# Two chunks of a two-layer kernel: written-out engine lists, a projection loaded in quarters, and two small matmul groups placed elsewhere

## The chip, the cores and the metric

The kernel runs on one core of one Trainium2 chip. The metric is the device time of one execution in microseconds (us). The program's engines run side by side, each through its own list of instructions in order: TensorE (PE, with its weight loads as PEld), VectorE (DVE), ScalarE (ACT), GpSimd (POOL) and SyncE (SP, which here only issues transfers).

## The reference

A residual stream x of 16 x 256 tokens with 256 features goes through two layers, all in float32. The first layer, where the whole change lies, is:

```
xn = layernorm(x)
s  = recurrence(xn)                      # B projection, complex decay over 256 steps,
                                         # C projection, plus D * xn
g  = silu(gelu(xn @ proj1.T + b1) @ proj2.T + b2)
x  = x + s * g
```

The hidden width is 1024 and the recurrence has 32 complex states per sequence; its B is scaled by a gain, its decay and angle come from two small parameter vectors. The second layer has the same frame, with multi-head latent attention (16 heads, causal) as s and a routed low-rank projection as g.

## The kernel before

The 4096 tokens are cut into 8 chunks of 512, that is two sequences, and x stays in SBUF for the whole run. Layer 0 goes chunk by chunk:

- `norm0` makes xn (statistics and the final scaling on VectorE, the power -0.5 on GpSimd as `rs`), `turn0` transposes it on TensorE to `xnT`.
- `hidden` makes the 8 blocks of the first projection (`ph` in PSUM) from `p1T` and `xnT`; ScalarE takes each through Gelu to `hT`. The PSUM pool `ps_mm` has four buffers, so TensorE can run four blocks ahead of ScalarE.
- `recur` multiplies by the turned B (`bT`) into `pb`, and VectorE and GpSimd run the scan to `hs`.
- `mix` makes half of the second projection (`pf`, two PSUM buffers), VectorE adds the bias to get `zf`, ScalarE applies Silu.
- `outs` multiplies `hs` by `csc` into two PSUM buffers `py` (pool `ps_y`, two buffers in all), GpSimd makes `dx = xn * D`, and VectorE adds `py` to it. `finish0` multiplies by `zf` and adds to x, on GpSimd.
- `fold_heads` folds weights of layer 1 (matmuls `psq` and `pso`) in the first four chunks.

The first chunk is special. `start` loads x in four pieces, computes statistics and projections by halves of the chunk, and interleaves VectorE's long list of tiny operations that make the recurrence's parameters (`later.write`): from `par` the exponent, the angle and the gain; then `gsq` (a square root as a power, on GpSimd), `gs`, the scaled B `bsc`, then `rot`, `ct`, `stb`, `sns`, `decay`, `csc`. `turn_b` transposes `bsc` into `psb` and ScalarE copies it to `bT`.

TensorE's order is always the order in which the program is written (`pe` is an `InOrder`, whose call helper is line 53, so most instructions are shown there). In the first chunk VectorE (`v0`), GpSimd (`g0`), ScalarE (`a0`) and SyncE (`s0`) have such lists too, but not for every instruction: those written on `nc.scalar`, `nc.gpsimd` or `nc.vector` directly are placed by a scheduler. In the program before, the order around the change is: on TensorE `pf` of chunk 0 first half, `psb`, `pf` second half, `ph` of chunk 1, `pb`, and so on; on ScalarE both Silus of chunk 0 ahead of the eight Gelus of chunk 1; on GpSimd the four copies `wrope<-wraw` of `load_layer1` (line 147) ahead of `gsq`; in chunk 1 `py` of chunk 0, the transposes of chunk 2, `py` of chunk 1, then the second half of `pf`.

Of the kernel before, what the change touches and what calls it, by code (L numbers as in the profile page):

```python
# [11 lines left out]
F32 = mybir.dt.float32  # L12
I32 = mybir.dt.int32
AF = mybir.ActivationFunctionType
ALU = mybir.AluOpType
# [3 lines left out]
P = 128  # L19
B, S, D = 16, 256, 256  # L20
# [5 lines left out]
FF = 1024  # L26
# [15 lines left out]
def tile_two_layers(ctx: ExitStack, tc: tile.TileContext, d: dict, out: bass.AP):  # L42
    nc = tc.nc
# [96 lines left out]
    rb_bc = w1.tile([P, NE], F32, tag="rb_bc", name="rb_bc")  # L140
    kvw_bc = w1.tile([P, KVL], F32, tag="kvw_bc", name="kvw_bc")

    def load_layer1(wraw):
        nc.sync.dma_start(wraw, d["wq_rope"].rearrange("(c p) n f -> p c n f", p=P))
        for c in range(2):
            for r in range(2):
                nc.gpsimd.tensor_copy(
                    wrope[:, c, :, r, :, :],
                    wraw[:, c, :, HR * r : HR * r + HR].rearrange("p (g h) f -> p g h f", h=4),
                )  # L150
        nc.sync.dma_start(wkva, d["wkv_a"].rearrange("(c p) f -> p c f", p=P))
        nc.sync.dma_start(wmid, d["w_mid"].rearrange("(c p) f -> p c f", p=P))
        nc.sync.dma_start(wbase, d["base_wT"].rearrange("(c p) f -> p c f", p=P))
        nc.sync.dma_start(wlb, d["lora_B"])
        nc.sync.dma_start(bb_bc, d["base_b"].partition_broadcast(P))
        nc.sync.dma_start(rb_bc, d["router_b"].partition_broadcast(P))
        nc.sync.dma_start(kvw_bc, d["kv_norm_w"].partition_broadcast(P))

        nc.sync.dma_start(rot_q[0:64, 0, :], d["rope_q"][0:64, 1, :])
        nc.sync.dma_start(rot_q[64:128, 0, :], d["rope_q"][64:128, 0, :])  # L160
        for h in range(4):
            nc.sync.dma_start(rot_q[32 * h : 32 * h + 32, 1, :], d["rope_q"][32:64, 2, :])
        nc.sync.dma_start(rope_k, d["rope_k"])
        nc.sync.dma_start(desc, d["desc"])
# [33 lines left out]
    def bc(ap, n):  # L198

        return ap.unsqueeze(1).to_broadcast([ap.shape[0], n, ap.shape[1]])  # L200
# [6 lines left out]
    with ExitStack() as l0:  # L207
# [3 lines left out]
        a2 = l0.enter_context(tc.tile_pool(name="a0", bufs=2))  # L211
# [5 lines left out]
        wraw = stage.tile([P, 2, NH, ROPE], F32, tag="wraw", name="wraw", bufs=1)  # L217
        p1T = w0.tile([P, 2, FF], F32, tag="p1T", name="p1T")
        p2T = w0.tile([P, NFC, D], F32, tag="p2T", name="p2T")
        b1 = w0.tile([P, NFC], F32, tag="b1", name="b1")  # L220
        b2_bc = w0.tile([P, D], F32, tag="b2_bc", name="b2_bc")
        d_bc = w0.tile([P, D], F32, tag="d_bc", name="d_bc")
# [5 lines left out]
        p1d = d["proj1T"].rearrange("(c p) f -> p c f", p=P)  # L228
        p2d = d["proj2T"].rearrange("(c p) f -> p c f", p=P)
        s0 = InOrder(nc.sync)  # L230
        a0 = InOrder(nc.scalar)
        a0.dma_start(par, d["par"])
        a0.dma_start(b1, d["proj1_b"])
        for j in range(TPC):
            s0.dma_start(X[0][:, j, :], x_dram[j * P : (j + 1) * P, :])
        for z, e in ((0, a0), (1, s0)):
            fz = slice(z * FF // 2, (z + 1) * FF // 2)
            e.dma_start(p1T[:, :, fz], p1d[:, :, fz])
        a0.dma_start(sgn, d["signs"])
        s0.dma_start(bst, d["B_stack"][0 : 2 * NST, :])  # L240
        load_x(1, s0)
# [25 lines left out]
        g0 = InOrder(nc.gpsimd)  # L267
# [72 lines left out]
        f = tiny("f")  # L340
# [12 lines left out]
        for k in range(1, 8):  # L353
            c, s = rot[:, k - 1, 0:1], rot[:, k - 1, 1:2]
# [10 lines left out]
        for k in range(8):  # L365
            n = 1 << k
            c, s = rot[:, k, 0:1], rot[:, k, 1:2]
# [63 lines left out]
        def hidden(ch, xnT):  # L431
            hT = []
            for fc in range(NFC):
                ph = ps_mm.tile([P, CH], F32, tag="mm", name=f"ph_{ch}_{fc}")
                for c in range(2):
                    pe.matmul(
                        ph, p1T[:, c, fc * P : (fc + 1) * P], xnT[:, c, :],
                        start=(c == 0), stop=(c == 1),
                    )
                ht = hpool.tile([P, CH], F32, tag="hT", name=f"hT_{ch}_{fc}")  # L440
                nc.scalar.activation(ht, ph, AF.Gelu, bias=b1[:, fc : fc + 1])  # L441
                hT.append(ht)
            return hT

# [9 lines left out]
        def recur(ch, xnT):  # L454

            pb = ps_mm.tile([P, S], F32, tag="mm", name=f"pb_{ch}")
            for c in range(2):
                for b in range(2):
                    pe.matmul(
                        pb[64 * b : 64 * b + 64, :], bT[:, c, :],  # L460
                        xnT[:, c, b * S : (b + 1) * S], start=(c == 0), stop=(c == 1),
                    )

            v = a2.tile([P, S], F32, tag="v", name=f"v_{ch}")
            w = a2.tile([P, S], F32, tag="w", name=f"w_{ch}")
            v0.tensor_tensor(v, pb, ct, ALU.mult)
            swapped(w, pb)
            nc.gpsimd.tensor_tensor(v, v, w, ALU.add)
            g = a2.tile([P, S], F32, tag="g", name=f"g_{ch}")
            nc.vector.tensor_tensor_scan(g, decay, v, 0.0, ALU.mult, ALU.add)  # L470
            swapped(w, g)
            h = a2.tile([P, S], F32, tag="hs", name=f"hs_{ch}")
            nc.vector.tensor_tensor(h, g, ct, ALU.mult)
            nc.gpsimd.tensor_tensor(h, h, w, ALU.subtract)
            return h

        def mix(ch, jp, hT):
            pf = ps_f.tile([P, 2, D], F32, tag="pf", name=f"pf_{ch}_{jp}")
            for j2 in range(2):
                cols = slice((2 * jp + j2) * P, (2 * jp + j2 + 1) * P)  # L480
                for fc in range(NFC):
                    pe.matmul(
                        pf[:, j2, :], hT[fc][:, cols], p2T[:, fc, :],
                        start=(fc == 0), stop=(fc == NFC - 1),
                    )
            zf = a2.tile([P, 2, D], F32, tag="zf", name=f"zf_{ch}_{jp}", bufs=3)
            nc.vector.tensor_tensor(zf, pf, bc(b2_bc, 2), ALU.add)
            nc.scalar.activation(zf, zf, AF.Silu)
            return zf

        def outs(ch, h, xn):

            py = [
                ps_y.tile([P, 2, D], F32, tag="py", name=f"py_{ch}_{b}") for b in range(2)
            ]
            for j2 in range(2):
                for b in range(2):
                    rows = slice(64 * b, 64 * b + 64)
                    pe.matmul(
                        py[b][:, j2, :], h[rows, j2 * P : (j2 + 1) * P], csc[rows, :],  # L500
                        start=True, stop=True,
                    )
            dx = []
            for b in range(2):
                dx.append(a2.tile([P, 2, D], F32, tag="dx", name=f"dx_{ch}_{b}", bufs=4))
                (nc.gpsimd if ch else g0).tensor_tensor(
                    dx[b], xn[:, 2 * b : 2 * b + 2, :], bc(d_bc, 2), ALU.mult
                )
                nc.vector.tensor_tensor(dx[b], py[b], dx[b], ALU.add)
            return dx  # L510

        def finish0(ch, jp, dx, zf):
            js = slice(2 * jp, 2 * jp + 2)
            nc.gpsimd.tensor_tensor(dx[jp], dx[jp], zf, ALU.mult)
            nc.gpsimd.tensor_tensor(X[ch][:, js, :], X[ch][:, js, :], dx[jp], ALU.add)
# [77 lines left out]
            return xn, xnT, hT, xn2, xnT2  # L593

        xn, xnT, hT, xn2, xnT2 = start()
        for ch in range(NCH):
            if ch > 1:
                hT = hidden(ch, xnT)
            if ch == 0:

                zf = [mix(ch, 0, hT)]
                turn_b()
                zf.append(mix(ch, 1, hT))
                xn3 = norm0(2)
                hT = hidden(1, xnT2)
                g = recur(ch, xnT)
                fold_heads(ch)
                g0_, xn0, zf0 = g, xn, zf
            else:
                if ch == 1:  # L610
                    xn2 = xn3
                elif ch + 1 < NCH:
                    xn2 = norm0(ch + 1)
                g = recur(ch, xnT)
                if ch < NH // HG:
                    fold_heads(ch)
                if ch == 1:
                    zf = mix(ch, 0, hT)
                    dx = outs(0, g0_, xn0)
                    for jp in range(2):  # L620
                        finish0(0, jp, dx, zf0[jp])
                if ch + 1 < NCH:
                    xnT2 = turn0(ch + 1, xn2)
                if ch > 1:
                    zf = mix(ch, 0, hT)
                dx = outs(ch, g, xn)
                finish0(ch, 0, dx, zf)
                zf = mix(ch, 1, hT)
                finish0(ch, 1, dx, zf)
            xn, xnT = xn2, xnT2  # L630


# [606 lines left out]
```

## Time and profile before

| What | Value |
|---|---|
| Median of three runs | 962.02 us (960.08 to 964.19) |
| Profiled execution, whole time | 960.92 us |
| Span of its instructions | 959.2 us, so 1.7 us lie around it |
| TensorE busy | 932.9 us (97% of the span) |
| VectorE, ScalarE, GpSimd busy | 64%, 44%, 44% |
| Mean granted TensorE clock | 0.993 |

Layer 0 ends near 283 us, the rest is layer 1. An engine's share of busy time is a mean over stages with different limits; here the first 87 us are a stage by themselves, in which TensorE stands idle several times, while from there to the end of layer 0 it is hardly ever idle.

### The profile page before, as it was taken

How to read it: one execution, taken by the hardware profiler on the slowest of the kernel's cores; microseconds unless marked ns; L12 is line 12 of the kernel's file. 1: busy time of each engine (PE TensorE's matmuls, PEld its weight loads, DVE VectorE, ACT ScalarE, POOL GpSimd, SP SyncE). 2: the span in 40 equal slices, each digit the busy share in tenths (PEclk: the TensorE clock that was granted, in tenths of full speed). 3: DMA queues.
4: the chain of work that ended last, by engine and by line, in shares of the span. 5: the costliest groups of instructions: out<-in, count | busy, mean ns of one | idle time of the engine just before them, and what ended most of it. 6: DMA issues, size and time to landing. Idle time of an engine off the chain costs nothing.

```text
span 959.2 us, 15744 instructions
## 1 busy us (share of the span) xinstructions
PE 932.9 (97%) x4778; PEld 669.5 (70%) x4778; DVE 614.8 (64%) x1943; ACT 426.7 (44%) x1420; POOL 422.1 (44%) x750
## 2 busy tenths in 40 slices
PE   8889999999989899999999999999999999999988
PEld 7656756775666566677777777777777776777776
DVE  6673433442146878967867886786788679677562
ACT  3132233223315555544554554554456455446540
POOL 1136224422243544554554455445455544546440
PEclk9999999999999999999999999999999999999999
DMA  9630000000002677686677677678777767767760
GB/s 292 198 108 3 1 1 0 1 1 1 0 1 45 135 208 220 171 221 171 173 202 193 165 186 212 173 185 201 180 187 181 205 173 177 209 168 186 227 196 29
DMA packets 196309, 133.90 MB, mean 140 GB/s; under 512 B 142272, under 2 KB 186624, under 8 KB 196224
## 3 DMA queue, kind: packets, MB, share of 16 engines
q1 hardware_dynamic: 194176, 128.68, 51.3%
q0 software_dynamic: 1344, 3.67, 1.0%
q8 instruction: 39, 0.64, 0.3%
q10 hardware_dynamic: 704, 0.53, 0.2%
q14 instruction: 46, 0.38, 0.1%
HBM read 63.11 MB, written 52.95 MB: 121 GB/s over the span
## 4 chain that ended last, share of the span: by engine, by line
PE 86%; DVE 6%; DMA 3%; POOL 2%; SPq 1%; issue 1%; ACT 1%; ACTq 0%; DVEq 0%; POOLq 0%
PE pq L53 21%; PE sc L53 14%; PE po L53 11%; PE pf L53 10%; PE ph L53 10%; PE av L53 9%; PE pg L53 4%; PE pm L53 1%; PE pkv L53 1%; POOL pr L53 1%; PE tp L53 1%; DMA wraw<-in_wq_rope_dram 1%; PE py L53 1%; SPq L53 1%; PE pb L53 1%; DVE w L53 1%
## 5 line engine op out<-in xcount | busy, mean ns | idle before, releaser
L53 ACT ACTIVATE pr<-sc,nm 128x256 f32<-128x256 f32 (+7 forms) x512 | 189.9, 380 | 284.4 <-DVE sr L53 192.6
L53 POOL TENSOR_SCALAR pr<-pr,sr 128x256 f32<-128x256 f32 (+7 forms) x512 | 193.3, 398 | 274.6 <-DVE sr L53 265.7
L53 PEld LDWEIGHTS sc<-kT,qg 128*128 128x128 f32 x1024 | 160.2, 191 | 63.6 <-issue 39.1
L53 PE MATMUL sc<-kT,qg 128*128 128x256 f32 (+7 forms) x1024 | 176.9, 307 | 5.8 <-DMA qg<-qrot 4.1
L53 DVE STREAM_TRANSPOSE turned<-pr 128x512 f32<-128x512 f32 x186 | 123.3, 688 | 15.3 <-POOL pr L53 15.1
L53 DVE TENSOR_REDUCE nm<-sc 128x1 f32<-128x256 f32 (+7 forms) x512 | 127.7, 301 | 6.6
L53 PE MATMUL pq<-xnT,wlat 128*128 128x512 f32 x256 | 125.6, 615 | 0.0
L53 PE MATMUL pq<-xnT,wrope 128*128 128x512 f32 x256 | 120.1, 593 | 0.0
L53 PE MATMUL ph<-xnT,p1T 128*128 128x512 f32 (+1 forms) x288 | 113.5, 552 | 6.1 <-ACT hT L441 4.6
L53 PE MATMUL po<-wout,attT 128*128 128x256 f32 x512 | 115.8, 380 | 0.0
L53 PE MATMUL pf<-p2T,hT 128*128 128x256 f32 x512 | 114.2, 381 | 0.0
L53 PEld LDWEIGHTS po<-wout,attT 128*128 128x128 f32 x512 | 96.4, 190 | 20.9 <-issue 6.4
L53 PEld LDWEIGHTS pf<-p2T,hT 128*128 128x128 f32 x512 | 96.0, 190 | 15.6 <-issue 2.4
L53 ACT ACTIVATION_READ_ACCUMULATOR pr<-sc,nm 128x1 f32 x512 | 103.4, 202 | 0.0
L53 PEld LDWEIGHTS ph<-xnT,p1T 128*128 128x128 f32 x288 | 55.1, 192 | 60.0 <-issue 49.7
L53 PE MATMUL av<-pT,row 128*64 128x256 f32 (+1 forms) x1024 | 90.5, 329 | 0.1
L53 POOL TENSOR_TENSOR qrot<-qmul,qmul 128x512 f32<-128x512 f32 x64 | 83.1, 1321 | 15.4 <-DVE sc L53 11.5
L53 DVE TENSOR_TENSOR qmul<-pq,rot_q 128x512 f32<-128x512 f32 x128 | 80.8, 673 | 0.0
L53 PEld LDWEIGHTS av<-pT,row 128*64 128x64 f32 x1024 | 64.2, 137 | 22.7 <-issue 0.5
L53 ACT ACTIVATE qg<-pq 64x512 f32<-64x512 f32 x128 | 75.5, 590 | 8.0 <-PE pq L53 7.2
L53 DVE TENSOR_TENSOR sc<-sc,kmask 128x96 f32<-128x96 f32 (+1 forms) x192 | 45.8, 239 | 49.3 <-PE sc L53 48.1
L53 PEld LDWEIGHTS pq<-xnT,wlat 128*128 128x128 f32 x256 | 46.8, 195 | 33.2 <-issue 33.2
(163 smaller groups left out, 905.5 us busy)
## 6 DMA issues: line engine op xcount, KB each, us to landing
far<-turned SPq DMA_DIRECT2D x248, 192.0 KB, 3.6
pT<-far SPq DMA_DIRECT2D x62, 768.0 KB, 4.8
qg<-qrot SPq DMA_DIRECT2D x256, 64.0 KB, 2.3
x<-in_x_dram SPq DMA_DIRECT2D x7, 512.0 KB, 8.8
out_dram<-o POOLq DMA_DIRECT2D x28, 128.0 KB, 3.2
wqn<-in_wq_nopeT_dram SPq DMA_DIRECT2D x4, 512.0 KB, 4.5
wo<-in_Wo_dram SPq DMA_DIRECT2D x4, 512.0 KB, 5.7
p2T<-in_proj2T_dram SPq DMA_DIRECT2D x2, 512.0 KB, 7.4
```

Of the source, the lines that this page charges most:

```text
L53: r = getattr(self.engine, name)(*args, **kw)
```

## The change

It does five things, in the first two chunks alone.

- The first half of `p1T`, on ScalarE's queue, is loaded in two quarters, and the first goes out ahead of `b1` and `par`; `par` becomes third.
- The four copies to `wrope` leave `load_layer1` and stand, in GpSimd's written-out list, behind `gsq`; the load of `wraw` itself keeps its place on SyncE's queue.
- `turn_b` stands behind both halves of `mix` of chunk 0 instead of between them.
- ScalarE's list goes on through chunk 1: the Gelus of chunk 1 come first, then both Silus of chunk 0.
- `dx = xn * D` is a function of its own (`direct`), called for chunk 0 ahead of `norm0(2)`; in chunk 1 the second half of `mix` stands ahead of `outs`, and both calls of `finish0` behind it.

The built programs differ in this order: on GpSimd `gsq`, the four copies, the four `dx` of chunks 0 and 1, then `rs` of chunk 2 (before: the copies, `gsq`, `rs` of chunk 2, the four `dx`); on ScalarE one load of an activation table fewer and one transfer more; on VectorE only the bias add of chunk 1's second half, now ahead of the two adds of `py`; on SyncE nothing.

```diff
+    def spread_rope(wraw, g):
         for c in range(2):
             for r in range(2):
-                nc.gpsimd.tensor_copy(
+                g.tensor_copy(
                     wrope[:, c, :, r, :, :],
...
+        def load_p1(e, f0, f1):
+            e.dma_start(p1T[:, :, f0:f1], p1d[:, :, f0:f1])
+
+        load_p1(a0, 0, FF // 4)
+        a0.dma_start(b1, d["proj1_b"])
         a0.dma_start(par, d["par"])
-        a0.dma_start(b1, d["proj1_b"])
+        load_p1(a0, FF // 4, FF // 2)
         for j in range(TPC):
             s0.dma_start(X[0][:, j, :], x_dram[j * P : (j + 1) * P, :])
-        for z, e in ((0, a0), (1, s0)):
-            fz = slice(z * FF // 2, (z + 1) * FF // 2)
-            e.dma_start(p1T[:, :, fz], p1d[:, :, fz])
+        load_p1(s0, FF // 2, FF)
         a0.dma_start(sgn, d["signs"])
...
-                nc.scalar.activation(ht, ph, AF.Gelu, bias=b1[:, fc : fc + 1])
+                (a0 if ch == 1 else nc.scalar).activation(
+                    ht, ph, AF.Gelu, bias=b1[:, fc : fc + 1]
+                )
...
-            nc.scalar.activation(zf, zf, AF.Silu)
+            if ch:
+                nc.scalar.activation(zf, zf, AF.Silu)
             return zf
...
+        def direct(ch, xn, g=nc.gpsimd):
+
+            dx = []
+            for b in range(2):
+                dx.append(a2.tile([P, 2, D], F32, tag="dx", name=f"dx_{ch}_{b}", bufs=4))
+                g.tensor_tensor(dx[b], xn[:, 2 * b : 2 * b + 2, :], bc(d_bc, 2), ALU.mult)
+            return dx
...
         xn, xnT, hT, xn2, xnT2 = start()
+        spread_rope(wraw, g0)
...
-                zf = [mix(ch, 0, hT)]
+                zf = [mix(ch, jp, hT) for jp in range(2)]
                 turn_b()
-                zf.append(mix(ch, 1, hT))
+                dx0 = direct(0, xn, g0)
                 xn3 = norm0(2)
                 hT = hidden(1, xnT2)
+                for z in zf:
+                    a0.activation(z, z, AF.Silu)
                 g = recur(ch, xnT)
                 fold_heads(ch)
...
                 if ch == 1:
                     zf = mix(ch, 0, hT)
-                    dx = outs(0, g0_, xn0)
+                    outs(0, h0, dx0)
                     for jp in range(2):
-                        finish0(0, jp, dx, zf0[jp])
+                        finish0(0, jp, dx0, zf0[jp])
                 if ch + 1 < NCH:
                     xnT2 = turn0(ch + 1, xn2)
...
+                if ch == 1:
+                    zf = [zf, mix(ch, 1, hT)]
+                    dx = direct(ch, xn)
+                    outs(ch, g, dx)
+                    for jp in range(2):
+                        finish0(ch, jp, dx, zf[jp])
+                else:
+                    dx = direct(ch, xn)
+                    outs(ch, g, dx)
+                    finish0(ch, 0, dx, zf)
+                    zf = mix(ch, 1, hT)
+                    finish0(ch, 1, dx, zf)
```

## The prediction

> **What bounds the kernel now.** I read the page first. TensorE is busy 97% of the span, and it carries most of the chain that ended last, so only time in which TensorE stands idle, or runs at a lower clock, is to be had.
>
> ```profile
> PE 932.9 (97%) x4778; PEld 669.5 (70%) x4778; DVE 614.8 (64%) x1943; ACT 426.7 (44%) x1420; POOL 422.1 (44%) x750
> PE 86%; DVE 6%; DMA 3%; POOL 2%; SPq 1%; issue 1%; ACT 1%; ACTq 0%; DVEq 0%; POOLq 0%
> ```
>
> Next the waits of TensorE over the whole run. Four of them lie in the first 80 us, where the change is (4.6, 1.5, 1.4 and 1.2 us).
>
> ```profile
> PE ph L53 <- ACT hT L441: 4.6, 1, 4.6
> PE py L53 <- DVE dx L509: 1.5, 1, 1.5
> PE ph L53 <- DMA p1T<-in_proj1T_dram: 1.4, 1, 1.4
> PE psb L53 <- DVE bsc L53: 1.2, 1, 1.2
> ```
>
> Then TensorE's timeline, to see what stands around them (start, length, instruction, idle time before it).
>
> ```profile
> 8.30 3.69 PE L53 MATMUL ph<-xnT,p1T 128*128 128x256 f32 x16 [1.43 <-DMA p1T<-in_proj1T_dram]
> ...
> 23.50 7.07 PE L53 MATMUL pf<-p2T,hT 128*128 128x256 f32 x32
> 31.78 0.30 PE L53 MATMUL psb<-ident,bsc 64*128 64x64 f32 x2 [1.20 <-DVE bsc L53]
> 32.01 7.17 PE L53 MATMUL pf<-p2T,hT 128*128 128x256 f32 x32
> 39.02 7.03 PE L53 MATMUL ph<-xnT,p1T 128*128 128x512 f32 x16
> 50.69 8.83 PE L53 MATMUL ph<-xnT,p1T 128*128 128x512 f32 x16 [4.64 <-ACT hT L441]
> ```
>
> The last two lines hold the same work; the second takes 1.8 us longer. The table of stretches says why: the granted clock there is 0.81 (columns: stretch, its length, busy PE, PEld, ACT, clock, DMA).
>
> ```profile
> 50.69:59.52 8.83, 8.83 (x16) 3.55 (x16) 3.74 (x6) 0.81 0.00 0
> 86.53:100.40 13.87, 13.87 (x32) 5.89 (x31) 4.81 (x7) 1.00 0.00 1
> ```
>
> Last, who makes those waits: the timelines of GpSimd, ScalarE and VectorE.
>
> ```profile
> 28.27 2.28 POOL L147 COPY wrope<-wraw 128x512 f32<-128x512 f32 x4 [11.99 <-DMA wraw<-in_wq_rope_dram]
> 30.51 0.54 POOL L53 TENSOR_TENSOR gsq<-gam,phalf 128x1 f32<-128x1 f32 x1
> ```
> ```profile
> 48.00 0.63 ACT L488 ACTIVATE zf<-zf 128x512 f32<-128x512 f32 x1 [7.30 <-DVE zf L487]
> 48.65 1.28 ACT L441 ACT_TABLE_LOAD   x1
> 49.95 2.42 ACT L441 ACTIVATE hT<-ph,b 128x512 f32<-128x512 f32 x4
> ```
> ```profile
> 6.92 0.43 DVE L53 BATCH_NORM_STATS2 st<-x 128x6 f32<-128x256 f32 x1 [1.01 <-DMA x<-in_x_dram]
> 7.39 0.18 DVE L53 BATCH_NORM_AGGREGATE mv<-st 128x2 f32<-128x6 f32 x1
> 7.49 0.66 DVE L53 COPY xnT<-tp 128x512 f32<-128x512 f32 x1
> ```
>
> The gain `gam` is ready at 22.0 us, but `gsq` stands behind copies that wait for `wraw` until 28.27. So `gs` and `bsc`, and the whole chain `rot` to `csc` behind them on VectorE, start 9.1 us late; `psb` stalls TensorE; the bias add of `zf` sits in that chain at 47.28; the Silu waits for it, and the Gelus of chunk 1 stand behind the Silu and a table load. TensorE has filled its four PSUM buffers and stops.
>
> **The change, part by part.**
>
> `gsq` ahead of the copies: it runs at 22.0, so `bsc` is there by about 23.1. VectorE's chain then waits only for the sine (24.8) instead of starting at 32.16, and `csc` ends near 43.9 instead of 51.2. The copies keep their time (28.27 to 30.5) and are first read at 280.67, so moving them costs nothing; without that cover it would be 2.28 us.
>
> `psb` behind the second `pf`: TensorE is gapless from 8.30 through both `pf`, 30.57 + 7.01 = 37.58. `bsc` is 14 us old by then. **-1.20**. The price of its place: `psb` now stands directly ahead of `hidden(1)`, and ScalarE's copy `bT` (0.27) and one table load (1.28) run from 37.9 to 39.5, while the first `ph` block is ready at about 39.6. Gelu needs 0.69 per block against TensorE's 1.72, so ScalarE never falls behind.
>
> Gelus ahead of Silus: the stall goes, **-4.64**, and with it the half clock after it: 16 matmuls at full clock are half of 13.73 (chunk 2's row in the chain), 6.87, so 8.83 becomes 6.87, **-1.96**. The two Silus and their table load (0.63 x 2 + 1.28 = 2.54 us) now run at about 52.5 to 55.0. Queued behind them on ScalarE is the copy of `pso`, which is ready at about 55.6; the reader of its PSUM buffer is the transpose of chunk 2, over 10 us later. Hidden; if not, 2.5 us on a buffer with that slack. Nobody reads `zf` of chunk 0 before about 69 us.
>
> `dx` early: four multiplies (2.49 + 2.54 us) now stand ahead of `rs` of chunk 2 on GpSimd, 30.5 to 35.6; `rs` is asked for only at about 45.7. There is one price. When GpSimd ran `dx` at 56.5, VectorE's four `xn` took 3.26 us instead of the 1.38 of another chunk. Applied to all 7.3 us of copies and `dx` beside VectorE's chain, at the same loss (1.88 per 2.54), that is 5.4 us. The chain ends (with `norm0(2)`) near 48.1, and `pb` comes at 51.6 and is read at 52.7, so 0.8 would be left over; the next matmul that wants a buffer from VectorE has 1.5 us of slack. So nothing, from 0 to 0.8 off the path.
>
> Second `pf` of chunk 1 ahead of `py`: before, `py` of chunk 1 waited 1.48 for VectorE to empty the two buffers, and took 1.64 instead of the 1.06 of other chunks, since the second buffer came later still. With 7.0 us of `pf` in front, both are free (the adds ended at 78.4, 2 us after the transposes). **-1.48 - 0.58**. What moves behind: VectorE's two adds and GpSimd's `finish0(1, ...)`, whose x is read in layer 1; ScalarE's last Silu of chunk 1 comes, seen from `ph` of chunk 2, 1.06 us sooner, so its Gelus are not late. The third `zf` buffer is free once GpSimd has done its first multiply, about 71 against a need at 76.
>
> Quarters: the wait of 1.43 is put down to `p1T` (landed 8.17), but the other input, `xnT`, ended at 8.15: the wait hides two causes, and the quarter removes only one. `xnT` waited for the third piece of x (6.92). At best that piece lands before the transposes end at 6.87, and `ph` starts at about 7.8: -0.5. Against it, 256 KB now travel with the first two pieces; at the page's 292 GB/s that is 0.90 us. The third piece shows what company costs: issued beside `p1T`, it landed 5.3 us after its issue, the first one, alone, 2.1. And `par` is third on its queue, needed at 4.17 in front of `xn`: with its 2.3 us from issue to landing it comes at 3.95 at the earliest; `sgn`, issued behind `p1T`, landed 1.83 after it, which behind a quarter landing at 4.3 makes 6.1, and `ph` 1.2 late. So -0.5 to +1.2; I take **+0.3**, nearer the row of the free transfers, since a quarter is half of what held up the third piece.
>
> The Trainium skill, page "DMA: Bandwidth & Descriptors", section "Issuing engines are not separate DMA queues", speaks against this edit: transfers of all issuing engines run on the same 16 DMA engines and interleave, and a second issuer saves only issue time. By that rule the head is at the late end, +0.9 instead of +0.3; the trace agrees with it as far as the third piece goes.
>
> The sum: -1.20 - 4.64 - 1.96 - 1.48 - 0.58 + 0.3 = **-9.6**. Behind 87 us TensorE's list is unchanged up to the end and every input moves with it, so the gain is carried through. On the profiled execution: 960.9 - 9.6 = 951.3. That execution lies 1.1 below the median of the three runs; the median of all four is 961.5, so I forecast **951.9**.
>
> **The rivals.**
>
> *The head falls to half clock.* If `par` or the first pieces come 1.7 late, TensorE idles 2.07 before its first transposes. Gaps of 1.43 and 1.48 left the clock at 1.00, gaps of 1.87 (at 925 us) and 2.00 (at 286 us) were followed by some 3.4 us near 0.5. So +1.2 and +1.96 instead of +0.3: 954.8. For: `sgn`'s landing. Against: b and `par` are tiny. Chance 0.14.
>
> The Trainium skill, page "TensorE: Matmul & The Clock Gate", Part 1, lets the clock fall only after at least one idle window of about 3.4 us. By that rule a head gap of 2 us is free and this rival ends at 952.8. The trace disagrees with it (2.00 us was enough), and the measurement decides.
>
> *Later clock dips vanish.* The two dips after the gaps of 1.87 and 2.00 are near the edge; 9.6 us earlier they could be missed, at 1.7 us each: 948.5. Chance 0.07.
>
> *A wait takes the stall's place.* ScalarE starts the Gelus late, because `psb` or `bT` is late, and half of the 6.6 stays: about 955 to 958. `bsc` would have to be later than 37.6, though even the old order had it at 31.6. Chance 0.03.
>
> *Slower: layer 1 loses its rhythm.* In layer 1 every unit moves `qg`, `far` and `pT` by DMA at a share of 0.7, and one such wait (4.1 us, `sc` on `qg`) is there. If each of 31 units lost over 0.31 us, the 9.6 would be gone; at 0.5 it is 967. Against: the lists of layer 1 are the same and TensorE's waits there are zero between 380 and 900 us. Chance 0.04.
>
> **How the numbers follow.** Forecast 0.72, and the four rivals 0.14, 0.07, 0.03, 0.04. The range: downward the better head (-0.8) and one dip less (-1.7), 949.4, taken as 949.0 for the spread of medians; upward the bad head with half clock and a little spread, 955.3. Outside are the slower case, half of the vanished dips and most of the third rival. A measurement of this kernel tells about 0.5% (4.8 us) from no change, so faster means under 957.2: 0.72 + 0.14 + 0.07 = 0.93; same 0.03; slower 0.04.
>
> **What would show it.** In the profile after: `gsq` near 22 us and `bsc` near 23; no wait of `psb`; `ph` of chunk 1 in one piece of 13.8 us at clock 1.00; `py` of chunk 1 without a wait; `ph` of chunk 2 starting near 77 instead of 86.53; the first `ph` between 7.8 and 9.5. Wrong would be a start of chunk 2's `ph` later than 80, a clock under 1.00 before 30 us, or a distance from there to the end that is more than 2 us longer than now.

## The result, and the profile after

The changed kernel takes 953.57 us (median of six executions, 951.76 to 954.57) against 961.69 (six, 959.28 to 964.19) of the kernel before on the same chip: a ratio of 0.9914, 95% interval 0.9894 to 0.9935. It is faster by more than half a per cent. The forecast of 951.9 was 1.7 us too low, with the time inside its range. The profiled executions stand at 952.76 against 960.92: -8.16, where the sum said -9.6.

The page of the changed kernel: TensorE's busy time has gone down by 1.0 us, the span by 8.2, so most of the gain is idle time removed. In the chain that ended last, TensorE's share goes from 86% to 93%.

```profile
PE 931.9 (98%) x4778; PEld 669.1 (70%) x4778; DVE 618.0 (65%) x1943; ACT 425.5 (45%) x1419; POOL 420.6 (44%) x750
PE 93%; DVE 3%; POOL 1%; DMA 1%; SPq 1%; ACT 1%; issue 0%; DVEq 0%; ACTq 0%; POOLq 0%
```

The waits of TensorE over the whole run (total, times, longest). The three waits of `ph` for `hT`, of `py` for `dx` and of `psb` for `bsc` are gone, and behind the head no line has taken their place. At the head two waits are left: the one ahead of the first transposes (`tp`) has grown from 0.37 to 1.44 us, and the one ahead of `ph` has shrunk from 1.43 to 0.79, with `xnT` as its releaser, where it was `p1T`.

```profile
PE tp L53 <- DVE xn L53: 1.6, 2, 1.4
...
PE ph L53 <- DVE xnT L53: 0.8, 1, 0.8
```

TensorE's timeline of the same kernel (start, length, instruction, idle time before it). From 8.36 us to the start of chunk 2's `ph` there is no idle time. The `ph` of chunk 1 is one piece of 14.00 us, at 39.45, where before it was 7.03 + 4.64 idle + 8.83. `py` of chunk 1, at 77.25, waits for nothing and takes 1.14.

```profile
6.71 0.87 PE L53 MATMUL tp<-ident,xn 128*128 128x128 f32 x4 [1.44 <-DVE xn L53]
8.36 5.41 PE L53 MATMUL ph<-xnT,p1T 128*128 128x256 f32 x16 [0.79 <-DVE xnT L53]
...
25.28 13.98 PE L53 MATMUL pf<-p2T,hT 128*128 128x256 f32 x64
39.19 0.33 PE L53 MATMUL psb<-ident,bsc 64*128 64x64 f32 x2
39.45 14.00 PE L53 MATMUL ph<-xnT,p1T 128*128 128x512 f32 x32
...
77.25 1.14 PE L53 MATMUL py<-csc,hs 64*128 64x256 f32 x8
78.31 14.00 PE L53 MATMUL ph<-xnT,p1T 128*128 128x512 f32 x32
```

The second line is what went otherwise than forecast: the first 16 matmuls take 5.41 us, before 3.69. The table of stretches (stretch, length, busy PE with its matmuls, granted clock, DMA share, GB/s) shows the clock below 1.00 at the head:

```profile
8.00:16.00 8.00, 7.64 (x30) 0.79 1.00 292
```

Chunk 2's `ph` starts at 78.31, 8.22 earlier. From there to the end of the span it is 951.0 - 78.31 = 872.69 us; before it was 959.2 - 86.53 = 872.67. What the first two chunks gained arrived at the end whole.

GpSimd's timeline after: `gsq` stands in front of the copies and waits for nothing but the gain; the copies still wait for `wraw`, and `dx` of both chunks follows.

```profile
23.65 0.55 POOL L53 TENSOR_TENSOR gsq<-gam,phalf 128x1 f32<-128x1 f32 x1 [5.83 <-DVE gam L53]
28.73 2.27 POOL L53 COPY wrope<-wraw 128x512 f32<-128x512 f32 x4 [4.53 <-DMA wraw<-in_wq_rope_dram]
30.97 2.49 POOL L53 TENSOR_TENSOR dx<-xn,d_bc 128x512 f32<-128x512 f32 x2
```

VectorE's timeline after, at the head and beside `dx`. The first two pieces of x come at 3.39 and 4.49, before at 2.83 and 3.42. And operations on a single column take 1.2 us while GpSimd multiplies.

```profile
3.39 0.43 DVE L53 BATCH_NORM_STATS2 st<-x 128x6 f32<-128x256 f32 x1 [3.39 <-DMA x<-in_x_dram]
...
4.49 0.43 DVE L53 BATCH_NORM_STATS2 st<-x 128x6 f32<-128x256 f32 x1 [0.45 <-DMA x<-in_x_dram]
```
```profile
31.05 1.20 DVE L53 SCALAR_TENSOR_TENSOR f<-rot,u 128x1 f32<-128x1 f32 x1
32.28 0.15 DVE L53 TENSOR_SCALAR f<-f 128x1 f32<-128x1 f32 x1
...
33.52 1.18 DVE L53 TENSOR_TENSOR u<-rot 128x1 f32<-128x1 f32 x1
```

### The profile page after: what moved, and what is told of

Its sections match the earlier page's. It is cut to its first block, busy times and chain, and to the rows that moved or that the text cites. A ratio compares the mean times of both kernels' runs of the same rounds, so it can differ in the third digit from the quotient of the medians.

```text
span 951.0 us, 15739 instructions
## 1 busy us (share of the span) xinstructions
PE 931.9 (98%) x4778; PEld 669.1 (70%) x4778; DVE 618.0 (65%) x1943; ACT 425.5 (45%) x1419; POOL 420.6 (44%) x750
## 3 DMA queue, kind: packets, MB, share of 16 engines
q0 software_dynamic: 1344, 3.67, 1.0%
## 4 chain that ended last, share of the span: by engine, by line
PE 93%; DVE 3%; POOL 1%; DMA 1%; SPq 1%; ACT 1%; issue 0%; DVEq 0%; ACTq 0%; POOLq 0%
PE pq L53 22%; PE sc L53 15%; PE ph L53 12%; PE pf L53 12%; PE po L53 11%; PE av L53 9%; PE pg L53 4%; PE pm L53 2%; PE tp L53 1%; PE pkv L53 1%; PE py L53 1%; PE pb L53 1%; PE psq L53 1%; POOL pr L53 1%; DVE nm L53 1%; SPq L53 1%
```

## The experiments

Twelve runs, in three groups of four; the runs of a group share a chip and the executions of the kernel before. First three variants of the changed kernel and one of the kernel before, all about the head.

**The old loads in the changed kernel.**

```diff
-        load_p1(a0, 0, FF // 4)
-        a0.dma_start(b1, d["proj1_b"])
         a0.dma_start(par, d["par"])
-        load_p1(a0, FF // 4, FF // 2)
+        a0.dma_start(b1, d["proj1_b"])
+        load_p1(a0, 0, FF // 2)
```

> The changed kernel with the loads of before (par, b1, then the first half of p1T in one piece). Theory: the quarter in front costs the head 1.8 us (two pieces of x land 0.6 and 1.1 us later, and the idle time they make drops the clock for 3.4 us), so without it the first projection starts at 8.3, its first 16 matmuls take 3.7 us instead of 5.4, the projection of chunk 2 starts near 76.6 instead of 78.3, and the time is 951.8. Rival: the lower clock at the head is a matter of chance and has nothing to do with the loads; then the time stays at 953.6.

Measured: 952.15 us (949.83 to 953.55), 0.9906 of the kernel before (0.9888 to 0.9924). In its profile the first piece of x comes at 2.87 again, and the head of TensorE's timeline is

```profile
7.63 3.72 PE L53 MATMUL ph<-xnT,p1T 128*128 128x256 f32 x16 [0.78 <-DVE xnT L53]
```

so earlier by 0.73 and quicker by 1.69; `ph` of chunk 2 starts at 75.89, 2.4 earlier. The times do not part the theory from its rival, since 0.9906 here and 0.9914 for the changed kernel have intervals that overlap; and some of the kernels below have the old loads and a slow head all the same, so the loads do not answer for the lower clock alone. The profile also shows that the head in the profile of the kernel before (8.30) was a late one of its kind: with the same loads the wait for `p1T` is not there.

**Quarters, but behind `par` and `b1`.**

```diff
-        load_p1(a0, 0, FF // 4)
-        a0.dma_start(b1, d["proj1_b"])
         a0.dma_start(par, d["par"])
+        a0.dma_start(b1, d["proj1_b"])
+        load_p1(a0, 0, FF // 4)
         load_p1(a0, FF // 4, FF // 2)
```

> The changed kernel with the quarters kept, but in the old order: par, b1, first quarter, second quarter. It parts the place of the load from its size. Theory (the place costs): pieces one and two of x land as before the change (2.8 and 3.4 us), the first quarter is there before xnT, the first projection starts at 8.2 or earlier at full clock, 951.7. Rival (the quarters themselves, as smaller packets, hold up the pieces of x): the third piece lands no earlier than 6.9, the clock falls as in the changed kernel, 953.6.

Measured: 950.59 us (949.41 to 954.45), 0.9898 (0.988 to 0.9917). The pieces of x come at 2.92 and 3.48 again, as with the old loads, so it is the place in front that delays them. The first `ph` starts at 7.33, but in the profiled execution it takes 5.41, the half clock again, although the gaps in front of it were only 0.77 and 0.78. That it starts 0.3 before the `ph` of the undivided load is not shown to be the work of the cut: the transposes ahead of it start at 5.67 here and at 5.62 there, but take 0.87 instead of 1.23. The place of the load costs, a gain from its size is not shown, and the clock is a matter beside both.

**The new loads, with 13 warming matmuls instead of 8.**

```diff
-NWARM = 8
+NWARM = 13
```

> The changed kernel with 13 instead of 8 warming matmuls ahead of the first transposes, which fill 1.1 of the 1.44 us of idle time there. Theory: it is TensorE's idle time that drops the clock, so the first 16 matmuls of the projection take 3.7 instead of 5.4 us although their inputs come as late as in the changed kernel; 951.9. Rival: the clock falls for another reason, or the 0.8 us gap behind the transposes is enough; 953.6.

Measured: 950.54 us (949.74 to 954.06), 0.9898 (0.9881 to 0.9916). The pieces of x come as late as in the changed kernel (3.40 and 4.56), yet the clock holds:

```profile
8.44 3.72 PE L53 MATMUL ph<-xnT,p1T 128*128 128x256 f32 x16 [0.79 <-DVE xnT L53]
```

`ph` of chunk 2 starts at 76.70, 1.6 earlier than in the changed kernel: the 1.7 of the half clock, without the late inputs, which stay. One of the six executions, without a profile, took 954.06 all the same.

**The new loads alone, in the kernel before.**

```diff
+        load_p1(a0, 0, FF // 4)
+        a0.dma_start(b1, d["proj1_b"])
         a0.dma_start(par, d["par"])
-        a0.dma_start(b1, d["proj1_b"])
+        load_p1(a0, FF // 4, FF // 2)
...
-        for z, e in ((0, a0), (1, s0)):
-            fz = slice(z * FF // 2, (z + 1) * FF // 2)
-            e.dma_start(p1T[:, :, fz], p1d[:, :, fz])
+        load_p1(s0, FF // 2, FF)
```

> The kernel before with the new order of loads alone. Theory: the head loses the same 1.8 us, but the wait of psb (1.2 us) and the stall of the second chunk's projection, both set by VectorE's list behind the power on GpSimd and not by TensorE, swallow it: 961.7 to 962.2, no change. Rival (each part adds up by itself): 963.5.

Measured: 962.55 us (961.44 to 964.10), 1.0022 (1.0011 to 1.0033): slower by 1.9. My theory was that the stall of chunk 1 would swallow a late head, since its end hangs on `wraw`. That did not hold, and the likely reason is that `wraw` comes later too. In this profile the copies start here:

```profile
28.79 2.27 POOL L147 COPY wrope<-wraw 128x512 f32<-128x512 f32 x4 [9.43 <-DMA wraw<-in_wq_rope_dram]
```

Over all profiles that start is 27.6 on average with the old loads (eight profiles, 26.88 to 28.27) and 29.2 with the quarter in front (five, 28.12 to 30.26). It is SyncE's list that has slid: its load of `p1T`, which stands ahead of that of `wraw`, is issued at 4.14 here and at 4.08 in the changed kernel, before at 2.58. The two profiles show only 0.5 of the 1.9 us at the `ph` of chunk 2 (87.04 against 86.53); `wraw` was late in the profile of the kernel before as well (28.27).

The second group takes the other edits one at a time, each in the kernel before.

**The power ahead of the copies.** The four copies leave `load_layer1` and are written on `g0` behind `start()`; the rest is as before.

```diff
-                nc.gpsimd.tensor_copy(
...
         xn, xnT, hT, xn2, xnT2 = start()
+        for c in range(2):
+            for r in range(2):
+                g0.tensor_copy(
...
```

> The kernel before with one edit: the four copies to wrope stand behind the power gsq on GpSimd. Theory: this alone removes psb's wait and also the stall of the second chunk's projection, for VectorE's list comes 7 us earlier and with it the bias add and the Silu in front of the Gelus: 6.4 to 7.8 us less (VectorE's scaling of chunk 2 is slowed by GpSimd's dx beside it), 953.9 to 955.3. Rival (the sum in the prediction, which gave the 6.6 us of stall and clock to the new order of Gelus and Silus): only psb's 1.2 us, 960.5.

Measured: 955.48 us (953.04 to 957.88), 0.9939 (0.9916 to 0.9963): -5.6 by this edit alone, a little less than the 6.4 to 7.8 that theory gave. The wait of `psb` and the stall of `ph` are both gone, with Silu still written ahead of Gelu; but `py` of chunk 1 now waits longer than in the profile before (2.35 against 1.48), and the `pf` behind it is slow (8.16 against 7.17):

```profile
37.13 14.21 PE L53 MATMUL ph<-xnT,p1T 128*128 128x512 f32 x32
...
70.63 2.29 PE L53 MATMUL py<-csc,hs 64*128 64x256 f32 x8 [2.35 <-DVE dx L503]
72.84 8.16 PE L53 MATMUL pf<-p2T,hT 128*128 128x256 f32 x32
```

The reading by which this edit is worth the `psb` wait alone is out.

**The Gelus of chunk 1 ahead of the Silus.**

```diff
-                nc.scalar.activation(ht, ph, AF.Gelu, bias=b1[:, fc : fc + 1])
+                (a0 if ch == 1 else nc.scalar).activation(
+                    ht, ph, AF.Gelu, bias=b1[:, fc : fc + 1]
+                )
...
-            nc.scalar.activation(zf, zf, AF.Silu)
+            if ch:
+                nc.scalar.activation(zf, zf, AF.Silu)
...
                 hT = hidden(1, xnT2)
+                for z in zf:
+                    a0.activation(z, z, AF.Silu)
```

> The kernel before with one edit: the Gelus of chunk 1 stand ahead of the Silus of chunk 0 on ScalarE. Theory: the stall at 46 us is gone, but VectorE is as late as before (its list still starts at 31 us), so TensorE waits some 4 us for the buffer of pb instead, near 58 us; about 0.7 us less, 961.0. Rival (the sum in the prediction): 6.6 us less, 955.1.

Measured: 958.19 us (956.62 to 960.45), 0.9971 (0.9957 to 0.9985): -2.9. The stall of `ph` is gone here too, but a new wait stands on TensorE later on, between the weight foldings, with slow matmuls behind it:

```profile
61.36 3.40 PE L53 MATMUL psq<-wkb,wqn 128*128 128x64 f32 x16 [2.44 <-issue]
64.69 1.98 PE L53 MATMUL pso<-wo,wvb 128*64 128x256 f32 x8
66.59 8.08 PE L53 MATMUL pf<-p2T,hT 128*128 128x256 f32 x32
```

The profile names no releaser for it. By the order in which the four buffers of `ps_mm` go round, this `psq` takes the buffer of the first `pb`, and VectorE finishes reading that at 61.26; so it is the wait that theory expected, 2.4 us long instead of 4. In the profile chunk 2's `ph` starts 1.2 earlier than before. The size lies between what theory (-0.7) and the prediction's sum (-6.6) gave, so the edit is worth less than half of what was booked to it; the rest of the difference stays open, since the landing of `wraw` (27.65 here, 28.27 before) and the head's clock differ between executions.

**The second half of chunk 1 ahead of its `py`.** The loop of `mix`, `outs` and `finish0` for chunk 1 as in the change, the rest as before.

```diff
+                if ch == 1:
+                    zf = [zf, mix(ch, 1, hT)]
+                    dx = outs(ch, g, xn)
+                    for jp in range(2):
+                        finish0(ch, jp, dx, zf[jp])
```

> The kernel before with one edit: in chunk 1 the second half of the second projection stands ahead of its outputs py. Theory and prediction agree: the wait of 1.48 us and the 0.58 us of the stretched py go, whatever comes before, 2.06 us less, 959.6. Rival: VectorE, which sets that stretch, lets TensorE wait at the next place instead (the copy of xnT for chunk 2), and nothing is gained, 961.7.

Measured: 956.89 us (954.61 to 958.32), 0.9954 (0.9939 to 0.9969): -4.2, twice the 2.06 that was expected. In its profile `py` waits for nothing, while the stall of chunk 1 is still there (3.67, and 9.99 for the 16 matmuls behind it). The profile shows the gain that was expected, and no more: from the first `pb` to `ph` of chunk 2 it is 24.93 us here (59.30 to 84.23), before 27.08 (59.45 to 86.53), so 2.15 less. The other two us of the medians stay open. The executions of this kernel have a mean granted clock of 0.994, those of the kernel before beside them 0.992, which is about 2 us of the span by estimate. A longer wait of `py` in some executions of the old order, with a lower clock behind it, would fit: it is 1.48 in two profiles (the kernel before, the quarters alone) but 2.35 and 2.33 in two others (the power alone, B turned alone) and nothing in a fifth (the Gelu order alone), and behind the 2.35 the clock fell (0.86 between 70 and 82 us). No profile of the kernel before shows this.

**B turned behind both halves, alone.**

```diff
-                turn_b()
                 zf.append(mix(ch, 1, hT))
+                turn_b()
```

> The kernel before with one edit: B is turned behind both halves of the second projection. Theory: psb's wait of 1.2 us goes, and the stall behind it grows by as much, since its end is set by the bias add in VectorE's list at 47.3 us; no change, 961.7, and a stall of 5.8 us in the profile. Rival (the sum in the prediction, part by part): 1.2 us less, 960.5.

Measured: 960.30 us (956.44 to 962.99), 0.9994 (0.9978 to 1.001): nothing by itself, as expected. The detail expected for the profile did not come: the stall was 2.32 and not 5.8, with `wraw` landing at 27.12 and a slow head in front (6.72 for its 16 matmuls), so that TensorE arrived later at a stall that ended sooner.

The third group asks for the best version, and whether two edits are enough.

**Old loads and 13 warming matmuls.** The edits of the first and third experiment together.

> The changed kernel with the loads of before and 13 warming matmuls: both heads that were tried apart. Theory: pieces of x early (2.9 us) and no half clock in the first projection in any execution, so chunk 2's projection starts near 75.9 and stays there, 1.5 to 2.5 us less than the changed kernel beside it: about 950. Rival (the head's half clock is a matter of the gate's phase that more warming does not govern): as the old loads alone, the first 16 matmuls now and then at 5 to 7 us, 1 us less than the changed kernel at most.

Measured: 949.61 us (four executions, 949.10 to 950.16), 0.9901 (0.9886 to 0.9916). Beside it the changed kernel took 954.04 (951.76 to 958.72): no execution of the one overlaps with one of the other, and the medians lie 4.4 apart. It beats both kernels, and its times lie within 1.1 us.

```profile
7.90 3.72 PE L53 MATMUL ph<-xnT,p1T 128*128 128x256 f32 x16 [0.79 <-DVE xnT L53]
```

**`dx` of chunk 0 late again, in the changed kernel.**

```diff
-                dx0 = direct(0, xn, g0)
                 xn3 = norm0(2)
+                dx0 = direct(0, xn, g0)
```

> The changed kernel with dx of chunk 0 behind norm0(2) again, so that GpSimd's four dx no longer stand beside VectorE's list of tiny operations. Theory: the tiny operations run at 0.15 to 0.22 us instead of waiting up to 1.2 us beside each dx, and the list (csc) ends near 46.5 instead of 50.2, but the scaling of chunk 2 beside the dx is slower by 1.9 again; TensorE waits for neither, the time is that of the changed kernel within 0.5 us. Rival: VectorE was the one that TensorE nearly waited for, and the time changes by over 1 us, either way.

Measured: 953.05 us (952.47 to 956.28), 0.9945 (0.9928 to 0.9961), against 0.9945 for the changed kernel beside it: the medians are 1.0 us apart, the executions overlap, and no difference is shown. `csc` comes at 46.52 instead of 50.21, TensorE's waits are the same, and chunk 2's `ph` starts at 78.40 (78.44 in the changed kernel on this chip). So the early `dx` does cost VectorE 3.7 us, and all of it is covered.

**Two edits alone.** The kernel before with the power ahead of the copies, and the second half of chunk 1 ahead of its `py`.

> The kernel before with two edits alone: the copies to wrope behind the power, and in chunk 1 the second half of the second projection ahead of py. Theory: the parts overlap and these two carry the whole gain; Gelus ahead of Silus, B turned later and dx early add nothing beside them. Chunk 2's projection starts near 76.5, 1 to 2 us less than the changed kernel beside it, since the loads are the old ones. Rival (the other three edits carry a part of their own): the stall of chunk 1's projection or a wait of psb is back in the profile, and the time is 2 us or more above the changed kernel with the old loads.

Measured: 951.23 us (950.01 to 952.17), 0.9918 (0.9904 to 0.9932). Only the waits of the head are left on TensorE, though this head too ran at the lower clock (5.41 for its 16 matmuls):

```profile
38.70 13.90 PE L53 MATMUL ph<-xnT,p1T 128*128 128x512 f32 x32
...
77.46 14.00 PE L53 MATMUL ph<-xnT,p1T 128*128 128x512 f32 x32
```

These two carry the whole gain, and are 2.8 us ahead of all the edits together on the same chip. Part of the 2.8 is the loads, which are the old ones here. Beside all the other edits with the old loads, the first experiment (0.9906, on another chip), the intervals overlap, so it is not shown that the three edits left out here add anything or cost anything.

**The changed kernel once more, on the chip of this group.**

> The changed kernel once more, as it is, as the yardstick for the runs beside it on the same chip. All theories: 0.991 of the kernel before, and a head with the pieces of x at 3.4 and 4.5 us.

Measured: 954.04 us (ten executions, 951.76 to 958.72), 0.9945 (0.9928 to 0.9962); `ph` of the head at 8.49 for 5.41 us. The median is within 0.5 us of the first measurement; the ratio is not the 0.991 that was expected, since the kernel before was quicker on this chip (959.24).

## Why the prediction was right, and where it was wrong

**Right: the three waits go, and their gain is carried to the end.** The terms of `psb`, the stall and `py` add up to -9.86 on the profiled execution, and with +1.78 for the head instead of +0.3 the sum gives -8.1; measured were -8.16 in the span and -8.22 at chunk 2's start. So the head is the whole of the miss. The head's +1.78 is a start later by 0.06 and 1.72 of lower clock. What was named as proof of error partly came: the clock was under 1.00 ahead of 30 us, while `ph` of chunk 2 came before 80 and the distance to the end stayed.

**Wrong: the term "quarters, +0.3".** It was taken near the row of the free transfers. The right neighbour was the row of the third piece, and the rule from the Trainium skill, page "DMA: Bandwidth & Descriptors", section "Issuing engines are not separate DMA queues", spoke on the same side: a second issuer gains issue time, not bandwidth. The trace agrees: the first two pieces of x came 0.56 and 1.07 late. Against the heads of the other six profiles with the old loads and 8 warming matmuls (7.51 to 7.68) the changed kernel's two (8.36 and 8.49) are 0.7 to 1.0 late, where this rule gave +0.9; the forecast compared with a head that was itself late. The transposes ahead of it show the delay by itself: they start at 6.71 and 6.83, against 5.62 to 5.75 in all seven profiles with the old loads and 8 warming matmuls.

**Wrong: the threshold of the first rival.** The prediction put the price of a half clock at gaps from 1.87 us. Here gaps of 1.44 and 0.79 were followed by it, and in two experiments gaps of 0.77 and 0.78, and of 0.70 and 0.89. Gap size alone does not decide: two kernels with the old loads have the same gaps to a hundredth (0.36 and 0.78), one takes 3.72 for the 16 matmuls and the other 6.77. With 13 warming matmuls, 3.72 in both profiles. So what happened is the outcome of the first rival, given 0.14, from a smaller delay and so at a lower price than its +3.16.

The traces tell two ways into the half clock apart. Between the two gaps stand four transposes, the same work in every kernel; these lines have the shortest, median and longest of the four in ns, in the changed kernel, in the kernel before and in the Gelu order alone.

```profile
L53 PE MATMUL tp<-ident,xn x4: 272/300/328, 6.7 to 7.3; 128*128 128x128 f32 x4
L53 PE MATMUL tp<-ident,xn x4: 421/447/475, 5.6 to 6.4; 128*128 128x128 f32 x4
L53 PE MATMUL tp<-ident,xn x4: 421/448/476, 5.6 to 6.4; 128*128 128x128 f32 x4
```

Then stretches of one microsecond (columns as in the table above), two of the changed kernel and two of the Gelu order alone:

```profile
9.00:10.00 1.00, 1.00 (x5) 0.64 0.90 290
12.00:13.00 1.00, 1.00 (x5) 0.66 1.11 320
```
```profile
13.00:14.00 1.00, 1.00 (x4) 1.00 0.73 239
14.00:15.00 1.00, 1.00 (x8) 1.00 0.86 274
```

In the changed kernel the transposes ran fast, so the clock was up already; it fell 0.9 us after `ph` began, for 3.4 us. The other four profiles in which the 16 matmuls took 5.41 have fast transposes too. In the Gelu order alone the transposes ran slowly and the matmuls went on so until near 14 us: there the clock had not come up yet. The other three profiles with a slow head (5.26, 6.56 and 6.72) are of this kind. In the profile of the kernel before, and in those of the old loads and of the power alone, the transposes ran slowly and `ph` fast, so the clock came up between them. The gap of 1.43 there, which the prediction read as one that leaves the clock at 1.00, is the gap in which it rose, and says nothing about a fall. With 13 warming matmuls the clock came up during them and stayed. What sets the moment at which it comes up, these runs do not tell.

The Trainium skill, page "TensorE: Matmul & The Clock Gate", Part 1, lets the clock fall only after an idle window of about 3.4 us. The trace disagrees: the longest idle time between the warming matmuls and the fall is 1.44 us. The same part has the window run on its own, whatever the kernel does. That would fit the pair of equal gaps, and a fall in the midst of busy matmuls that lasts 3.4 us; what the window counts, no run here shows.

**Wrong: which edit removes the stall.** The sum booked 6.6 us to the Gelus ahead of the Silus. The power ahead of the copies does it alone (-5.6); the Gelu order alone brings 2.9 and a new wait. The section on what bounds the kernel had the whole chain, from `gsq` over the bias add to the Silu and the Gelus, but the sum charged the link nearest to the stall instead of the first one. The total is not harmed by it, since both edits were made; a forecast for either would have been wrong. The single edits, from the loads to B turned, measure +1.9, -5.6, -2.9, -4.2 and -0.8: -11.6 in sum, against -8.1 together; two of them remove the same stall, so it is counted twice.

**Right in the profiles, short in the medians: the term of `py`, -2.06.** From the first `pb` to `ph` of chunk 2 the changed kernel takes 24.93 us (53.38 to 78.31), before 27.08: 2.15 less. Alone the edit brings the same 2.15 in its profile and 4.2 between medians, and the difference stays open.

**Right in the outcome, wrong in the numbers: VectorE's chain.** `csc` was to end near 43.9; it started at 50.21 and ended at 50.56, 6.7 later. Of these, 3.7 are `dx` beside VectorE, by the experiment with the late `dx`, and about 1.8 the later head. The loss beside GpSimd belonged into the time of `csc`, then, and not only into the slack behind it: `pb` ended at 54.46 and its first reader on VectorE started at 54.78. The cover was thin, and it held. ScalarE was in time as worked out: `bT` and the table load ended at 41.12, and the first Gelu then still waited 0.35 for its block.

**The other rivals.** No wait took the stall's place, and layer 1 kept its rhythm (872.69 against 872.67). Both later dips of the clock are in this profile too (0.79 between 276 and 284 us, 0.76 between 915 and 922), so they did not vanish here; in the second profile of the same kernel the later one is missing (1.00 between 915 and 925), and what decides that is open.

## What to carry to other kernels

A small operation that feeds a long chain should not stand in an engine's list behind work that waits for a transfer; look for the first link of a chain that is late, not for the last one before the stall, and charge the gain there. Edits that remove the same wait do not add up, so price them one at a time and together. A load placed in front of the first inputs is paid by these inputs, though another engine issues it; idle time of TensorE at the head is better filled with a few more warming matmuls.

## What was unexpected of the hardware

**Tiny operations of VectorE wait for GpSimd's.** While GpSimd multiplied 128x512 tiles (1.25 us each), VectorE's operations on one or two columns with two inputs, or an input and a column of scalars, took 1.01 to 1.20 us, against 0.15 to 0.23 elsewhere; one with a single input and a constant stayed at 0.15. The Trainium skill, page "SBUF — State Buffer", section "Who interferes with whom", describes a shared port pair as an exclusive lock; the trace agrees in the length, about one GpSimd operation per VectorE operation.

**The head's clock is a lottery, and the clock column can miss it.** The same 16 matmuls of the head took 3.69 to 6.77 us in different profiles. The column reads 1.00 at the start of each of them, though the first warming matmuls take 421 ns and, in the kernels with 13 of them, the last ones 275. In the profile with 6.77 (the Gelu order alone) the table of stretches shows TensorE busy throughout, with 27 matmuls in 8 us, fewer than the 30 of the changed kernel at 0.79, and a granted clock of 1.00:

```profile
8.00:16.00 8.00, 8.00 (x27) 1.00 0.99 319
```

The time of a run goes with its granted clock elsewhere too: over 59 executions of the kernel before (956.6 to 965.0 us, mean clock 0.988 to 0.998) the correlation of the two is -0.72.
